# Attention in turns of four steps on 64x64 tiles, with the values' PSUM banks lent to the stages between turns

## The chip, the cores and the metric

One core of one Trainium2 chip. The metric is the device time of one execution in microseconds (us). Engines: PE (TensorE matmul), PEld (its weight loads, which overlap PE), DVE (VectorE), ACT (ScalarE), POOL (GpSimd), SP (DMA queue). PSUM is the memory for matmul results, shared out in banks; the program uses eight.

## The reference, cut to what matters

Layer 0 is a graph convolution with two batch norms over all batches; it is finished 880 us into the kernel and the change does not touch it. Then, for each of 16 batches of `x` (1024 x 256, fp32):

```python
x = layernorm(x + layer0(x))
fea = x.T; c = fea.mean(0)                         # per node
A = abs(abs(sigmoid(c[None] - c[:, None]) - .5) - .5) * 2
g = relu((fea @ (adj * (A + A.T) / 2)) * para)     # -> q, 4 heads of 64
k, v = split(x @ kv_w)
out = softmax(q @ k.T * scale) @ v                 # per head
x = layernorm(x + out)
```

## The kernel before

One instruction stream holds three batches at once: attention of batch b, the graph product, keys and values of b+1, the first layer norm of b+2. Attention of a batch is 16 *steps*. A step takes one pair of heads, one half of the queries (512) and two blocks of 128 keys; four steps make one output tile `o`. The tile names in the profile: `s` scores, `e` their exponentials (ACT), `acc` the sums of e (DVE), `o` the values product, `ot` its copy, `pd`/`dt` the denominators, `pr` their transposes, `pf`/`r` the transposed output and the last layer norm, `yt`/`py`/`px` the first layer norm and its transposes, `wg`/`pg` the graph product, `pk`, `pv` keys and values.

```python
ps_s = pool("ps_s", 2, space=PSUM)      # two tiles of two banks
ps_o = pool("ps_o", 1, space=PSUM)
ps_t = pool("ps_t", 3, space=PSUM)      # everything else
...
def scores(g):                          # contraction over HD = 64 rows
    for a in range(2):
        cb = 2 * cp + a
        t = ps_s.tile([P, 2, FB], F32, tag="s", name=f"s{g}_{a}")
        for h in range(2):              # two 64x128 tiles, one per head
            nc.tensor.matmul(t[:, h, :], kTs[b, pair][h * HD : (h + 1) * HD, ts(cb, P)],
                             qTs[b, pair, hf][h * HD : (h + 1) * HD, :], start=True, stop=True)
...
def attend(g):                          # 64 output columns per head
    for a in range(2):
        for h in range(2):              # two 128x64 tiles
            nc.tensor.matmul(O[b, hf, pair][h * HD : (h + 1) * HD, :],
                             vs[b][:, cb, pair * P + h * HD : pair * P + (h + 1) * HD],
                             E[g, a][:, h, :], start=(cb == 0), stop=(cb == NT - 1))
    if cp == NT // 2 - 1:
        nc.scalar.copy(t, O.pop((b, hf, pair)))
...
for k in range(KB // 2):                # pieces are put into eight slots a batch
    put(b, t + 1 + k, finish_a, b, hf * (KB // 2) + k)   # pf, r, statistics; POOL makes nm
    put(b, t + 2 + k, finish_b, b, hf * (KB // 2) + k)   # ACT: r <- r, nm, rs; store
...
put(b - 2, j + 1, bn2, b, j)            # ACT: yt <- yt
put(b - 2, j + 2, ln1_a, b, j)          # PE: py <- yt, then DVE
...
for t in ...:                           # a slot: s, block of pieces, s, o
    scores(g + 2); exps(g + 2)
    sums(g)
    for f, a in now:
        f(*a)                           # the slot's block of other stages
    sums(g + 1)
    scores(g + 3); exps(g + 3)
    for k in live:
        attend(k)                       # g and g + 1
```

The order of emission is the order on each engine.

Of the kernel before, what the change touches and what calls it, by code (L numbers as in the profile page):

```python
# [9 lines left out]
F32 = mybir.dt.float32  # L10
# [3 lines left out]
PSUM = bass.MemoryType.PSUM  # L14
DRAM = bass.MemoryType.DRAM

P = 128
# [5 lines left out]
def gnn_norm_attention_kernel(  # L23
# [16 lines left out]
    nc = tc.nc  # L40
    B, N, C = x.shape
    H = W1.shape[0]
    NT = N // P
    CT = C // P
    HT = H // P
    FB = 512
    NH = N // FB
    HD = C // HEADS
# [38 lines left out]
    with ExitStack() as l0:  # L87
# [29 lines left out]
        with ExitStack() as ph1:  # L117
# [9 lines left out]
            for i in range(0, NT, 2):  # L127
                t = hp.tile([P, 2, N], F32, tag="h", name=f"A{i}")
# [281 lines left out]
    def fast():  # L410
      with ExitStack() as fx:
        pool = lambda name, bufs, **k: fx.enter_context(tc.tile_pool(name=name, bufs=bufs, **k))
# [10 lines left out]
        sm = pool("sm", 6)  # L423
        rp = pool("rp", 2)
        ps_s = pool("ps_s", 2, space=PSUM)
        ps_o = pool("ps_o", 1, space=PSUM)
        ps_t = pool("ps_t", 3, space=PSUM)

        x1s, x1Ts, css, crows, mvs, wgs = {}, {}, {}, {}, {}, {}
        kTs, qTs, vs, S, E, ACC, O, OT, DT = {}, {}, {}, {}, {}, {}, {}, {}, {}  # L430
# [121 lines left out]
                nc.vector.tensor_scalar(qs, qs, 0.0, scale, op0=OP.max, op1=OP.mult)  # L552


        def step(g):
            b, s = divmod(g, NS)
            hf, pair, cp = s // (NP * NT // 2), s // (NT // 2) % NP, s % (NT // 2)
            return b, hf, pair, cp

        def scores(g):  # L560
            b, hf, pair, cp = step(g)
            for a in range(2):
                cb = 2 * cp + a
                t = ps_s.tile([P, 2, FB], F32, tag="s", name=f"s{g}_{a}")
                for h in range(2):
                    nc.tensor.matmul(  # L566
                        t[:, h, :],
                        kTs[b, pair][h * HD : (h + 1) * HD, ts(cb, P)],
                        qTs[b, pair, hf][h * HD : (h + 1) * HD, :],
                        start=True,  # L570
                        stop=True,
                    )
                S[g, a] = t

        def exps(g):
            for a in range(2):
                E[g, a] = ep.tile([P, 2, FB], F32, tag="e", name=f"e{g}_{a}")
                nc.scalar.activation(E[g, a], S.pop((g, a)), AF.Exp)  # L578

        def sums(g):  # L580
            b, hf, pair, cp = step(g)
            if cp == 0:
                ACC[b, hf, pair] = accp.tile([P, 2, FB], F32, tag="acc", name=f"acc{g}")
                nc.vector.tensor_add(ACC[b, hf, pair], E[g, 0], E[g, 1])  # L584
            else:
                for a in range(2):
                    nc.vector.tensor_add(ACC[b, hf, pair], ACC[b, hf, pair], E[g, a])  # L587

        def attend(g):
            b, hf, pair, cp = step(g)  # L590
            if cp == 0:
                O[b, hf, pair] = ps_o.tile([P, FB], F32, tag="o", name=f"o{g}")
            for a in range(2):
                cb = 2 * cp + a
                for h in range(2):
                    nc.tensor.matmul(  # L596
                        O[b, hf, pair][h * HD : (h + 1) * HD, :],
                        vs[b][:, cb, pair * P + h * HD : pair * P + (h + 1) * HD],
                        E[g, a][:, h, :],
                        start=(cb == 0),  # L600
                        stop=(cb == NT - 1),
                    )
                E.pop((g, a))
            if cp == NT // 2 - 1:
                t = otp.tile([P, FB], F32, tag=f"ot{pair}", bufs=2 - pair, name=f"ot{g}")
                nc.scalar.copy(t, O.pop((b, hf, pair)))
                OT[b, hf, pair] = t

        def dens(b, hf):
# [83 lines left out]
        at = {}  # L693
# [7 lines left out]
        for b in range(B):  # L701

            for hf in range(NH):
                t = (hf + 1) * (NC // NH)
# [25 lines left out]
            for t, n in enumerate(KV):  # L730
                for _ in range(n):
                    f, a = kv.pop(0)
# [9 lines left out]
        nsteps = B * NS  # L742
# [4 lines left out]
        short = (dens, recips, finish_a, x1_t, ln1_a, crow)  # L747
        long = (keys, values, graph)

        def spread(few, many):  # L750

            res, done = [], 0
            for k, fa in enumerate(few):
                upto = len(many) * (k + 1) // (len(few) + 1)
                res += many[done:upto] + [fa]
                done = upto
            return res + many[done:]

        def arrange(pieces):
            first = [fa for fa in pieces if fa[0] is dens]  # L760
            gate = [fa for fa in pieces if fa[0] in (wg_a, wg_b)]
            many = [fa for fa in pieces if fa[0] in long]
            few = [fa for fa in pieces if fa not in first + gate + many]
            few.sort(key=lambda fa: rank.get(fa[0], len(rank)))
            few_pe = [fa for fa in few if fa[0] in short]
            order = spread(many, few_pe) if len(many) < len(few_pe) else spread(few_pe, many)
            if few_pe and many and order[0][0] in long:
                order.remove(few_pe[0])
                order.insert(0, few_pe[0])

            for fa in few:
                if fa[0] not in short:
                    at_ = 0
                    for k, o in enumerate(order):
                        if o[0] in rank and rank[o[0]] <= rank.get(fa[0], len(rank)):
                            at_ = k + 1
                    order.insert(at_, fa)
            pairs = [gate[k : k + 2] for k in range(0, len(gate), 2)]
            res = spread(order, pairs) if order else pairs
            flat = []  # L780
            for o in res:
                flat += o if isinstance(o, list) else [o]
            return first + flat

        for t in range(min(at), max(max(at), nsteps // 2 - 1) + 1):
            g = 2 * t
            now = arrange(at.get(t, []))
            live = [k for k in (g, g + 1) if 0 <= k < nsteps]
            ahead = [k for k in (g + 2, g + 3) if 0 <= k < nsteps]
            if ahead:  # L790
                scores(g + 2)
                exps(g + 2)
            while now and now[0][0] is dens:
                f, a = now.pop(0)
                f(*a)
            if live:
                sums(g)
            if not now and live:
                attend(g)
                live.pop(0)  # L800
                sums(g + 1)
            for f, a in now:
                f(*a)
            if now and live:
                sums(g + 1)
            if ahead:
                scores(g + 3)
                exps(g + 3)
            for k in live:
                attend(k)  # L810

        return nc.values_load(
            badi[0][0:1, 0:1],
# [3 lines left out]
        )  # L817

    flag = fast()


# [149 lines left out]
```

## Time and profile before

| | before |
|---|---|
| median of the first 3 runs | 2670.9 us (2669.99 to 2672.18) |
| PE busy | 2617.7 us, 98% of the span |
| DVE, ACT busy | 1383.0, 1213.4 us |
| one batch with all stages | 110.6 us, 13 of them; the first one took 108.8 |
| shared PSUM banks beside s and o | 3 |

"Busy" of PE is the union of matmul records, which overlap; the prediction therefore reads starts, not busy times. In a timeline row the columns are start, length of the merged group, engine, line, operation, tiles, shapes, count, and in brackets the idle time before it with what ended it. A matmul in fp32 leaves two records.

### The profile page before, as it was taken

Reading aid. Unit: us, or ns where it says so; the run is one execution under the profiler, and the core shown is the slowest. Engines: PE = TensorE matmul, PEld = TensorE weight load, DVE = VectorE, ACT = ScalarE, POOL = GpSimd, SP = SyncE. Lnnn points to the kernel's source line nnn. Section 1 sums busy time; section 2 is a strip of 40 time slices with the busy share of each in tenths; the row PEclk is TensorE's granted clock in tenths of the full one; section 3 lists DMA queues with packets and bytes.
Section 4 is the critical chain, followed back from the end, with each engine's and each line's share of the span. In section 5 each row is a group of like instructions: output and inputs, shape, how many; then the busy total and the mean of one; then the engine's idle time right before and its main releaser. Section 6 shows DMA issues by size and latency. Waiting matters only on the chain.

```text
span 2669.0 us, 24421 instructions
## 1 busy us (share of the span) xinstructions
PE 2617.7 (98%) x9081; PEld 1117.4 (42%) x9081; DVE 1383.0 (52%) x2198; ACT 1213.4 (45%) x1635; POOL 331.5 (12%) x464
## 2 busy tenths in 40 slices
PE   8999999999998899999999999999999999999997
PEld 4444444444444444443444434444344443444432
DVE  5222222223222465765757657576575765757556
ACT  2111111114554464564655646556465564655634
POOL 1110111000000100210102101021011110111102
PEclk9999999999999999999999999999999999999999
DMA  3212222222863111011010100101100011010000
GB/s 126 95 72 84 81 95 79 79 110 71 322 226 113 34 38 32 28 46 39 24 32 28 52 32 24 32 28 52 32 24 32 28 52 32 24 32 28 20 8 25
DMA packets 93789, 161.10 MB, mean 60 GB/s; under 512 B 7656, under 2 KB 73824, under 8 KB 86752
## 3 DMA queue, kind: packets, MB, share of 16 engines
q1 hardware_dynamic: 93664, 159.48, 17.1%
q8 instruction: 73, 1.20, 0.2%
q14 instruction: 52, 0.43, 0.1%
HBM read 97.53 MB, written 61.93 MB: 60 GB/s over the span
## 4 chain that ended last, share of the span: by engine, by line
PE 90%; DVE 5%; ACT 2%; issue 2%; DMA 0%; POOL 0%; SPq 0%; DVEq 0%; ACTq 0%; POOLq 0%
PE s L566 16%; PE pg L546 16%; PE o L596 15%; PE pa L263 14%; PE po L361 8%; PE ph L284 8%; PE pk L520 4%; PE pv L531 2%; PE px L470 1%; PE pd L615 1%; PE pa L247 1%; PE py L447 1%; DVE acc L587 1%; DVE wg L512 1%; DVE r L640 1%
## 5 line engine op out<-in xcount | busy, mean ns | idle before, releaser
L578 ACT ACTIVATE e<-s 128x1024 f32<-128x1024 f32 x512 | 499.0, 1021 | 577.1 <-PE o L596 414.9
L566 PE MATMUL s<-qT,kT 64*128 64x512 f32 x2048 | 508.9, 615 | 0.5 <-ACT e L578 0.5
L587 DVE TENSOR_TENSOR acc<-acc,e 128x1024 f32<-128x1024 f32 x384 | 469.6, 1223 | 19.6 <-DVE acc L587 1.4
L546 PE MATMUL pg<-wg,x 128*128 128x512 f32 x1024 | 467.2, 593 | 1.7 <-DVE wg L512 1.4
L596 PE MATMUL o<-e,v 128*64 128x512 f32 x2048 | 467.7, 598 | 0.0
L566 PEld LDWEIGHTS s<-qT,kT 64*128 64x128 f32 x2048 | 176.0, 186 | 307.4 <-issue 183.0
L303 ACT COPY hT<-ph 128x512 f32<-128x512 f32 x128 | 75.0, 586 | 453.7 <-PE ph L284 453.7
L596 PEld LDWEIGHTS o<-e,v 128*64 128x64 f32 x2048 | 135.5, 136 | 316.5 <-issue 315.4
L546 PEld LDWEIGHTS pg<-wg,x 128*128 128x128 f32 x1024 | 181.3, 190 | 174.6 <-issue 170.3
L512 DVE SCALAR_TENSOR_TENSOR wg<-wg,adj_sb 128x1024 f32<-128x1024 f32 x128 | 156.4, 1222 | 149.5 <-ACT wg L508 145.7
L284 PE MATMUL ph<-agg,W1T 128*128 128x512 f32 x512 | 222.2, 592 | 0.0
L361 PE MATMUL po<-hL,W2T 128*128 128x512 f32 x432 | 185.6, 592 | 0.0
L66 POOL TENSOR_SCALAR rs_z<-mv_z 128x2 f32<-128x2 f32 x64 | 24.0, 375 | 1097.4 <-DVE mv_z L402 1096.4
L304 DVE BATCH_NORM_STATS2 st<-ph 128x6 f32<-128x512 f32 x128 | 89.5, 699 | 136.6 <-ACT hT L303 136.6
L263 PE MATMUL pa<-T,sx 128*128 128x512 f32 x360 | 156.9, 592 | 0.0
L284 PEld LDWEIGHTS ph<-agg,W1T 128*128 128x128 f32 x512 | 97.3, 190 | 122.5 <-issue 122.2
L584 DVE TENSOR_TENSOR acc<-e,e 128x1024 f32<-128x1024 f32 x64 | 78.2, 1222 | 127.5 <-PE pd L615 127.5
L551 DVE TENSOR_TENSOR qT<-pg,para_sb 128x512 f32<-128x512 f32 x64 | 43.8, 684 | 192.7 <-PE pg L546 192.7
L365 DVE BATCH_NORM_STATS2 st<-po 128x6 f32<-128x512 f32 x64 | 44.7, 699 | 169.3 <-PE po L361 169.3
L361 PEld LDWEIGHTS po<-hL,W2T 128*128 128x128 f32 x432 | 82.1, 190 | 103.3 <-issue 103.3
L531 PE MATMUL pv<-kvw,x1T 128*128 128x256 f32 x512 | 121.7, 382 | 3.1 <-DVE r L640 3.1
L520 PE MATMUL pk<-x1T,kvw 128*128 128x512 f32 x256 | 116.9, 600 | 0.0
(133 smaller groups left out, 2475.6 us busy)
## 6 DMA issues: line engine op xcount, KB each, us to landing
h<-hT SPq DMA_DIRECT2D x27, 1024.0 KB, 3.8
hL<-h SPq DMA_DIRECT2D x27, 1024.0 KB, 8.7
x<-in_x_dram SPq DMA_DIRECT2D x16, 1024.0 KB, 5.0
yT<-y SPq DMA_DIRECT2D x32, 512.0 KB, 3.7
yt<-yT SPq DMA_DIRECT2D x64, 256.0 KB, 3.3
xr<-in_x_dram SPq DMA_DIRECT2D x64, 256.0 KB, 4.8
out_dram<-r SPq DMA_DIRECT2D x64, 256.0 KB, 2.1
crow<-crow_d SPq DMA_DIRECT2D x15, 512.0 KB, 4.1
```

Of the source, the lines that this page charges most:

```text
L263: nc.tensor.matmul(p, w[:, k, :], m[:, k, :], start=(k == 0), stop=(k == KN - 1))
L284: nc.tensor.matmul(p, W1T[:, k, ts(f, P)], aggT[b][:, k, ts(h, FB)], start=(k == 0), stop=(k == CT - 1),)
L304: nc.vector.bn_stats(st1[:, f, u, :], p)
L361: nc.tensor.matmul(po[c], W2T[:, k, ts(c, P)], hT[u][:, k, :], start=(k == 0), stop=(k == HT - 1))
L512: nc.vector.scalar_tensor_tensor(t, t, 1.0, adj_sb[:, i, :], op0=OP.add, op1=OP.mult)
L520: nc.tensor.matmul(p, kvw[:, k, ts(c, P)], x1Ts[b][:, k, ts(h, FB)], start=(k == 0), stop=(k == CT - 1))
L531: nc.tensor.matmul(p[:, ts(a, C)], x1Ts[b][:, k, ts(j + a, P)], kvw[:, k, C:], start=(k == 0), stop=(k == CT - 1),)
L546: nc.tensor.matmul(pg[b], x1s[b, k // 2][:, k % 2, ts(c, P)], wgs[b, k][:, ts(h, FB)], start=(k == 0), stop=(k == NT - 1))
L566: nc.tensor.matmul(t[:, h, :], kTs[b, pair][h * HD : (h + 1) * HD, ts(cb, P)], qTs[b, pair, hf][h * HD : (h + 1) * HD, :], start=True, sto ...
L578: nc.scalar.activation(E[g, a], S.pop((g, a)), AF.Exp)
L587: nc.vector.tensor_add(ACC[b, hf, pair], ACC[b, hf, pair], E[g, a])
L596: nc.tensor.matmul(O[b, hf, pair][h * HD : (h + 1) * HD, :], vs[b][:, cb, pair * P + h * HD : pair * P + (h + 1) * HD], E[g, a][:, h, :], ...
```

## The change

Its intent: s and o both use four 64x64 tiles, so that PE need not change its tile shape between them, and four steps stand together (a *turn*) behind one *block* of the other stages, so that shapes change only twice per turn. Each row half of the values product is given a bank of its own, and the halves are added (the prediction says why); the two banks come from the shared pool, which has them for the block.

```diff
-        ps_o = pool("ps_o", 1, space=PSUM)
-        ps_t = pool("ps_t", 3, space=PSUM)
+        ps_t = pool("ps_t", 4, space=PSUM)
 ...  (scores)
-                for h in range(2):
-                    nc.tensor.matmul(
-                        t[:, h, :],
-                        kTs[b, pair][h * HD : (h + 1) * HD, ts(cb, P)],
+                for r in range(2):
+                    for h in range(2):
+                        nc.tensor.matmul(
+                            t[r * HD : (r + 1) * HD, h, :],
+                            kTs[b, pair][h * HD : (h + 1) * HD, ts(2 * cb + r, HD)],
 ...  (attend)
-                O[b, hf, pair] = ps_o.tile([P, FB], F32, tag="o", name=f"o{g}")
+                O[b, hf, pair] = [ps_t.tile([P, FB], F32, tag="t", name=f"o{g}_{r}") for r in range(2)]
+                for r in range(2):
+                    for h in range(2):
+                        nc.tensor.matmul(
+                            O[b, hf, pair][r][h * HD : (h + 1) * HD, :],
+                            vs[b][r * HD : (r + 1) * HD, cb, pair * P + h * HD : pair * P + (h + 1) * HD],
+                            E[g, a][r * HD : (r + 1) * HD, h, :],
 ...
-                nc.scalar.copy(t, O.pop((b, hf, pair)))
+                o = O.pop((b, hf, pair))
+                nc.scalar.copy(t, o[0])
+                nc.vector.tensor_add(t, o[1], t)
 ...  (the loop; the old one goes)
+        NK = NT // 2
+        for t in range(min(at) // 2, max(max(at) // 2, nsteps // NK - 1) + 1):
+            g = NK * t
+            now = arrange(at.get(2 * t, [])) + arrange(at.get(2 * t + 1, []))
 ...         (the block, with sums(g) behind its last short PE piece)
+            for k in range(g, g + NK):
+                if 0 <= k + 1 < nsteps:
+                    scores(k + 1)
+                    exps(k + 1)
+                if 0 <= k < nsteps:
+                    if k > g:
+                        sums(k)
+                    attend(k)
```

More of the change, by code (lines that the diff above doesn't have):

```diff
@@ L564, in scores @@
                 t = ps_s.tile([P, 2, FB], F32, tag="s", name=f"s{g}_{a}")
-                for h in range(2):
-                    nc.tensor.matmul(
-                        t[:, h, :],
-                        kTs[b, pair][h * HD : (h + 1) * HD, ts(cb, P)],
-                        qTs[b, pair, hf][h * HD : (h + 1) * HD, :],
-                        start=True,
-                        stop=True,
-                    )
+                for r in range(2):
[3 more added lines that the diff above has]
+                            kTs[b, pair][h * HD : (h + 1) * HD, ts(2 * cb + r, HD)],
+                            qTs[b, pair, hf][h * HD : (h + 1) * HD, :],
+                            start=True,
+                            stop=True,
+                        )
                 S[g, a] = t
@@ L591, in attend @@
             if cp == 0:
-                O[b, hf, pair] = ps_o.tile([P, FB], F32, tag="o", name=f"o{g}")
+                O[b, hf, pair] = [ps_t.tile([P, FB], F32, tag="t", name=f"o{g}_{r}") for r in range(2)]
             for a in range(2):
                 cb = 2 * cp + a
-                for h in range(2):
-                    nc.tensor.matmul(
-                        O[b, hf, pair][h * HD : (h + 1) * HD, :],
-                        vs[b][:, cb, pair * P + h * HD : pair * P + (h + 1) * HD],
-                        E[g, a][:, h, :],
-                        start=(cb == 0),
-                        stop=(cb == NT - 1),
-                    )
+                for r in range(2):
[4 more added lines that the diff above has]
+                            E[g, a][r * HD : (r + 1) * HD, h, :],
+                            start=(cb == 0),
+                            stop=(cb == NT - 1),
+                        )
                 E.pop((g, a))
@@ L783, in arrange @@
             return first + flat
-        for t in range(min(at), max(max(at), nsteps // 2 - 1) + 1):
-            g = 2 * t
-            now = arrange(at.get(t, []))
-            live = [k for k in (g, g + 1) if 0 <= k < nsteps]
-            ahead = [k for k in (g + 2, g + 3) if 0 <= k < nsteps]
-            if ahead:
-                scores(g + 2)
-                exps(g + 2)
-            while now and now[0][0] is dens:
-                f, a = now.pop(0)
-                f(*a)
-            if live:
-                sums(g)
-            if not now and live:
-                attend(g)
-                live.pop(0)
-                sums(g + 1)
-            for f, a in now:
-                f(*a)
-            if now and live:
-                sums(g + 1)
-            if ahead:
-                scores(g + 3)
-                exps(g + 3)
-            for k in live:
-                attend(k)
+        NK = NT // 2
+        for t in range(min(at) // 2, max(max(at) // 2, nsteps // NK - 1) + 1):
+            g = NK * t
+            now = arrange(at.get(2 * t, [])) + arrange(at.get(2 * t + 1, []))
+            behind = max((k + 1 for k, fa in enumerate(now) if fa[0] in short), default=0)
+            for k in range(len(now) + 1):
+                if k == behind and 0 <= g < nsteps:
+                    sums(g)
+                if k < len(now):
+                    f, a = now[k]
+                    f(*a)
+            for k in range(g, g + NK):
[6 more added lines that the diff above has]
+                    attend(k)
         return nc.values_load(
```

## The prediction

> **What bounds the kernel now.** I read the page first. Its first part and its chain of waits agree on one engine:
>
> ```profile
> PE 2617.7 (98%) x9081; PEld 1117.4 (42%) x9081; DVE 1383.0 (52%) x2198; ACT 1213.4 (45%) x1635; POOL 331.5 (12%) x464
> ...
> PE 90%; DVE 5%; ACT 2%; issue 2%; DMA 0%; POOL 0%; SPq 0%; DVEq 0%; ACTq 0%; POOLq 0%
> PE s L566 16%; PE pg L546 16%; PE o L596 15%; PE pa L263 14%; PE po L361 8%; PE ph L284 8%; PE pk L520 4%; PE pv L531 2%; PE px L470 1%; PE pd L615 1%; PE pa L247 1%; PE py L447 1%; DVE acc L587 1%; DVE wg L512 1%; DVE r L640 1%
> ```
>
> PE bounds; no other engine passes 52%. But 98% busy means only that matmul records touch each other (ends are modelled), so what can be saved inside it must come from start times. The chain of waits in order of time shows pk coming back every 110.6 us from 1046.74 to 2484.51: that is one batch of attention together with the other stages of the next two. Fourteen such batches from 937.91 take 1546.6 us. Before 880 us the change touches nothing.
>
> The windows of one batch (second row) and of the last two, which have less beside attention:
>
> ```profile
> 1267.92:1378.52 110.60, 110.37 (x443) 45.94 (x442) 70.60 (x112) 61.57 (x80) 15.35 (x24) 1.00 0.11 34
> 2484.45:2591.06 106.61, 106.61 (x413) 42.77 (x409) 60.43 (x74) 55.21 (x67) 12.59 (x16) 1.00 0.03 10
> 2591.06:2652.00 60.94, 60.02 (x276) 20.32 (x272) 45.53 (x58) 32.99 (x41) 16.94 (x16) 1.00 0.05 18
> ```
>
> Columns: window, its us, busy PE, PEld, DVE, ACT, POOL, clock, DMA. The clock is full. Now the PE timeline of two of a batch's eight slots:
>
> ```profile
> 1273.20 1.99 PE L566 MATMUL s<-qT,kT 64*128 64x512 f32 x8
> 1275.12 3.65 PE L596 MATMUL o<-e,v 128*64 128x512 f32 x16
> 1278.70 1.99 PE L566 MATMUL s<-qT,kT 64*128 64x512 f32 x8
> 1280.62 0.66 PE L626 MATMUL pr<-ident,dt 128*128 128x128 f32 x4
> 1281.11 1.88 PE L520 MATMUL pk<-x1T,kvw 128*128 128x512 f32 x4
> 1282.83 1.89 PE L531 MATMUL pv<-kvw,x1T 128*128 128x256 f32 x8
> 1284.56 0.60 PE L637 MATMUL pf<-ident,ot 128*128 128x128 f32 x4
> 1285.00 1.89 PE L531 MATMUL pv<-kvw,x1T 128*128 128x256 f32 x8
> 1286.82 1.99 PE L566 MATMUL s<-qT,kT 64*128 64x512 f32 x8
> ```
>
> Read the differences of starts. pk: 1282.83-1281.11 = 1.72 for 4 records, 0.43 each. s: 8 records in 1.92; o: 16 in 3.58. Two records of s (two row halves) and two of o (two column halves) run at once, so s ought to take 4 x 0.43 = 1.71 and o 8 x 0.43 = 3.43. It costs **0.21 us more for each s group, 0.15 to 0.17 for o**, and the block of 128x128 work between them pays about 0.15 (the last pv 1.82 instead of 1.73; pr 0.49 instead of the 0.44 of pf). That is the price of leaving one tile shape and filling the next: about 0.1 out, 0.05 to 0.1 in.
>
> **What the Trainium skill says.** "TensorEngine Tiling (Array Packing)", section Tiling Modes: a change of mode, not of tile, drains the engine; 64x64 gives four tiles that may run together. The trace agrees on the first: every change of form above has its tenth or two, and none stands inside a group. No run yet shows the second for 64x64, but the pd matmuls are four tiles of 128x32:
>
> ```profile
> 1319.80 1.07 PE L615 MATMUL pd<-acc,ones 128*32 128x512 f32 x8
> 1320.80 0.33 PE L470 MATMUL px<-ident,x 128*128 128x128 f32 x1
> ```
>
> Eight records in 1.00 us are two rounds of four and a drain, so four at once works. The same page, section Restrictions and Gotchas: different row tiles must not use one PSUM bank at the same time. That is why the changed values product needs two banks and an addition. "Perfetto Trace Analysis", section Per-engine timelines: ScalarE and VectorE are strict FIFO. The timeline of ACT agrees (an e is done only after the wg and yt work issued before it), and my main worry rests on it.
>
> **The change part by part.** *Removed:* mode changes. A batch now has eight slots of s, block, s, o (twice as many steps as slots): s in and out twice, o once, block once, 0.21+0.21+0.16+0.15 = 0.73, times 8 = 5.8 us. Afterwards s and o are both 64x64 and four steps stand together; a batch has four turns, each with one change in and one out, about 0.29, so 1.2 us. **Saved 4.6 us a batch.** Check: the pure work of a batch is 64 rounds for s, 64 for o, 64 records for pg, 16 for pk (each 0.429: 89.2), 32 for pv (0.216: 6.9), 57 transposes (0.109: 6.2), pd 4 rounds (1.7), 104.0 in all; 110.6 - 104.0 = 6.6, of which the 5.8 is most.
>
> *Added on PE:* 2048 s and 2048 o records more, each a quarter of the array: 16 records of 0.43 us, four at once, take the 1.71 of 8 records two at once. Zero if four do run together, issue included: a round asks for four weight loads and four matmuls in 0.43 us, and the early transposes (30 in 3.56 us at 12.58, less as the clock rises) keep about 0.11 us per pair.
>
> *Added on DVE:* 64 additions from PSUM, 128x512. Row L449, the same kind of addition from PSUM, has 0.68 us, so 44 us of DVE, 1383 to 1427, beside PE. *ACT:* unchanged in work. *PSUM:* eight banks as before, but four for s and four shared in place of four, three shared and one for o; between turns the two of o serve the block. At a block's start one or two of them are free, and o's pair comes free after the ACT copy (0.59) and the DVE addition (0.69), some 1.6 us in, when the order of instructions first asks for them about 1 to 2.8 us in. Hidden, or nearly.
>
> *Moved, and this is where gain is given back:* two slots' pieces are now one block, with no attention between a piece that ACT prepares and the piece that PE does with it. I walked the orders of PE, ACT and DVE through the four blocks with the traced durations (ACT: copy 0.5, 256-wide 0.5, wg even 2.15, wg odd 1.05, e 1.0 when back to back).
> - Block B (second of a batch). PE: pf 0.5, pv 1.73, py 0.44, pv 1.73, done at 4.5, and then py of the next half slot, whose yt comes from ACT. ACT before that: ot to 0.7, two r to 1.7, v not before pv is done at 2.5, to 3.05, wg to 5.2, two yt to 6.3. With its four transposes PE is done at 6.7 instead of 4.9: **1.8 us of stall**. Before, a whole s-o-s stretch lay between.
> - Block A (first). PE 12.4 us (pd, 4 pk, pr, pf, 2 pv). ACT idles while it waits for pk and pv copies, then after the first v (10.85) has wg 2.15, yt 1.0, v 0.5, wg 1.05, so the first e of the turn is done at 16.55, where the second s of the turn wants its bank at 15.9: **0.8 us**.
> - Blocks C and D: ACT has only copies; the DVE chains (L640, L645, statistics, L456) end before PE asks. About 0.
> - Inside a turn: s for step k+1 is 1.71, o for step k 1.71, and e has over 1.2 us of slack. DVE sums 2.5 us a step against 3.42. About 0.
>
> So 2.6 given back, against some 0.4 of small stalls in a batch now: net 110.6 to about 108.1, -2.5. Times 14 = 35 us. Batch 15 (no py, no yt) keeps all 4.6, the last about 3 to 4 of it. The tail has one addition more, +0.7. Sum: 35 + 4.6 + 3.5 - 0.7 = 42, thus **2670.9 - 42 = 2629 us, -1.6%**.
>
> **The rivals.** (1) *The moved waits are hidden after all*: the gain is 4.6 to 5 in all 16 batches, 75 us, 2596. For it: the waits of the kernel before are tiny on PE, so the author's order is good. Against: block B's sum above is plain arithmetic on a FIFO. (2) *Four 64x64 tiles do not keep four at once*, because 2 x 18.7 instructions per us are not issued or fetched, or weight loads of one row half wait for each other. For: no run shows a long stretch of it; only the short pd and early transposes come near. Each 10% on the 55 us of s and o in a batch would be 5.5 us x 16 = 88 us, so 2715. Against: pd shows rounds of four at full pace, o and s each show the two halves free. (3) *PSUM becomes the wait*: o's two banks are held until DVE has added, and DVE is behind by its block work. A microsecond at each of 64 turns would be 64 us and cancel everything: 2690. Against: DVE in the walk is free within 1.5 us of each turn's end. (4) *ACT becomes the bound of whole turns*, if block A leaves it 3 us or more late: some 20 to 40 us more.
>
> **Range and chances.** The mode saving is firm (70 us if undisturbed); the give-back is 28 us by the walk, perhaps 0 to 60. That makes 2600 to 2668. Faster by over 2% needs under 2617.5, i.e. a give-back below about 18 us: 0.30. Slower by 2% needs rival 2: 0.07.
>
> **What would show it.** In the PE timeline of a batch, s and o should be one unbroken stretch of 13.7 us per turn, 128 records, with starts of a round 0.43 apart: the mode step and the four-at-once step. If it is longer with idle marked "issue", rival 2; if ended by ACT e inside the turn's first step, block A's estimate (or rival 4). A gap of about 1.8 us before py in the second block, ended by ACT yt, is the block B step; its absence makes me wrong towards 2600. Waits of PE for the DVE addition or the ACT copy of ot would be rival 3. The batch period should be near 108.1 us; 106 says rival 1, 110 or more says 2 or 3. DVE busy should rise by 44 us, ACT not at all, and nothing before 880 us should move.

## The result, and the profile after

| | before | after |
|---|---|---|
| median | 2671.54 us (4 runs) | 2641.41 us (4 runs; 2638.72 to 2642.31) |
| ratio | | 0.9886, 95% interval 0.9869 to 0.9903 |
| one batch | 110.60 us | 108.20 us |
| PE / DVE / ACT busy | 2617.7 / 1383.0 / 1213.4 | 2560.5 / 1426.4 / 1218.5 |

A ratio is the mean time of one kernel's fast runs over that of the other's of the same rounds, so not quite the ratio of the medians. The change gains 1.1%, clear of noise. All outputs are right.

From the page of the changed kernel (busy time by engine, and the chain that ended last by engine):

```profile
PE 2560.5 (97%) x13177; PEld 1114.8 (42%) x13177; DVE 1426.4 (54%) x2262; ACT 1218.5 (46%) x1635; POOL 346.4 (13%) x464
...
PE 90%; ACT 4%; DVE 3%; issue 1%; POOL 1%; DMA 0%; SPq 0%; ACTq 0%; DVEq 0%; POOLq 0%
```

PE has 4096 records more and still bounds; DVE is up by 43 us, as 64 additions should make it. ACT's share of the chain rises from 2% to 4%. Where it stands there, the PE timeline of the second block of a batch and of the ends of the turns around it tells:

```profile
1269.73 1.90 PE L599 MATMUL o<-e,v 64*64 64x512 f32 x16
1272.10 2.00 PE L568 MATMUL s<-qT,kT 64*64 64x512 f32 x16 [0.47 <-ACT e L580]
1273.91 1.90 PE L599 MATMUL o<-e,v 64*64 64x512 f32 x16
1275.63 1.90 PE L568 MATMUL s<-qT,kT 64*64 64x512 f32 x16
...
1282.61 0.66 PE L642 MATMUL pf<-ident,ot 128*128 128x128 f32 x4
1283.10 1.89 PE L530 MATMUL pv<-kvw,x1T 128*128 128x256 f32 x8
1284.83 0.60 PE L446 MATMUL py<-ident,yt 128*128 128x128 f32 x4
1285.27 1.89 PE L530 MATMUL pv<-kvw,x1T 128*128 128x256 f32 x8
1288.30 0.33 PE L446 MATMUL py<-ident,yt 128*128 128x128 f32 x1 [1.14 <-ACT yt L436]
1288.79 0.55 PE L446 MATMUL py<-ident,yt 128*128 128x128 f32 x3 [0.16 <-ACT yt L436]
```

Starts again: o 1273.91 to s 1275.63 is 1.72 us for 16 records, four rounds of 0.43 with nothing between o and s. Four tiles do run at once, and the change of shape inside the turn is gone. But s at 1272.10 came 0.65 us late by the starts (1269.73 + 1.72 is 1271.45; 0.47 of it shows as idle, for e) and py at 1288.30 came 1.3 us late: pv starts at 1285.27 and takes 1.73, so py could start at 1287.00. ACT's timeline of the same stretch:

```profile
1283.19 1.09 ACT L662 ACTIVATE r<-r,nm,rs_z 128x256 f32<-128x256 f32 x2
1285.03 0.59 ACT L537 COPY v<-pv 128x512 f32<-128x512 f32 x1 [0.75 <-PE pv L530]
1285.51 1.15 ACT L506 ACTIVATE wg<-crow,cs 128x1024 f32<-128x1024 f32 x1
1286.70 1.06 ACT L507 ACTIVATE wg<-wg 128x1024 f32<-128x1024 f32 x1
1287.66 1.08 ACT L436 ACTIVATE yt<-yt,t,s 128x256 f32<-128x256 f32 x2
```

ACT idles 0.75 us for pv, does 2.1 us of wg, and only then the yt that PE waits for. It is not short of time; it is a queue in an unlucky order.

To see where a batch's time goes I took, from the starts of its matmul records, the distance from each group of one tile to the next, less the pure work (0.429 us per record of 512 columns on the whole array, half or a quarter of that on two or four tiles, 0.216 for pv, 0.109 for a transpose). The pure work is 104.1 us in both kernels:

| extra in one batch, us | before | after |
|---|---|---|
| between s and o | 2.79 | 0.92 (about 0.7 of it goes with the late e) |
| from s or o to the block | 1.60 | 0.44 |
| from the block to s | 0.97 | 0.39 |
| waits for yt (before: of pv for a bank) | 0.40 | 1.68 |
| the rest (pd, fills inside the block) | 0.71 | 0.64 |
| sum | 6.47 | 4.07 |

That explains the full batches. It does not explain the end. In the span of the trace, the kernel is ahead by 2.1 us when the first of these batches starts, gains 4.4 in that one and 31.1 in the next 13 - 37.6 in all - and gives back 7.8 after 2446.85. The PE timeline of the last batch, where only short pieces are left between the turns:

```profile
2566.06 1.95 PE L568 MATMUL s<-qT,kT 64*64 64x512 f32 x16
2567.83 1.90 PE L599 MATMUL o<-e,v 64*64 64x512 f32 x16
2573.85 3.69 PE L568 MATMUL s<-qT,kT 64*64 64x512 f32 x16 [4.12 <-ACT e L580]
2577.31 2.84 PE L599 MATMUL o<-e,v 64*64 64x512 f32 x16
2579.98 1.89 PE L568 MATMUL s<-qT,kT 64*64 64x512 f32 x16
```

What ACT did meanwhile (timeline):

```profile
2571.80 1.09 ACT L662 ACTIVATE r<-r,nm,rs_z 128x256 f32<-128x256 f32 x2 [4.64 <-POOL nm L654]
2572.80 1.91 ACT L580 ACTIVATE e<-s 128x1024 f32<-128x1024 f32 x2
```

The clock of the two stretches from the window view; behind the window, its length and the busy times of PE, PEld, DVE, ACT and POOL stand granted clock, DMA share and GB/s:

```profile
2573.80:2580.00 6.20, 6.15 (x36) 1.94 (x40) 4.90 (x4) 2.96 (x3) 0.00 (x0) 0.56 0.12 42
2580.00:2587.00 7.00, 7.00 (x72) 2.18 (x68) 2.45 (x2) 3.88 (x4) 0.00 (x0) 1.00 0.00 0
```

ACT stood 4.64 us in front of an r whose nm POOL had not finished, with e behind it in the queue. PE idled 4.1 us, and then ran at half its clock (the 0.56 is a mean over a window that reaches past the slow stretch; the window 2572.40:2579.23 alone shows 0.50): s took 3.46 us from start to start in place of 1.72, the o after it 2.67. The same happens at 2607. Against whole turns at full clock the two places cost 7.0 and 6.7 us (idle 4.3 and 4.4, the rest the slow clock).

### The profile page after: what moved, and what is told of

The parts are those of the page before. It is cut to its first block, busy times and chain, and to the rows that moved or that the text cites. A ratio compares the mean times of both kernels' runs of the same rounds, so it can differ in the third digit from the quotient of the medians.

```text
span 2639.1 us, 32959 instructions
## 1 busy us (share of the span) xinstructions
PE 2560.5 (97%) x13177; PEld 1114.8 (42%) x13177; DVE 1426.4 (54%) x2262; ACT 1218.5 (46%) x1635; POOL 346.4 (13%) x464
## 3 DMA queue, kind: packets, MB, share of 16 engines
q8 instruction: 105, 1.72, 0.3%
## 4 chain that ended last, share of the span: by engine, by line
PE 90%; ACT 4%; DVE 3%; issue 1%; POOL 1%; DMA 0%; SPq 0%; ACTq 0%; DVEq 0%; POOLq 0%
PE pg L545 16%; PE s L568 16%; PE o L599 16%; PE pa L263 14%; PE po L361 8%; PE ph L284 8%; PE pk L519 4%; PE pv L530 1%; PE pd L620 1%; PE px L469 1%; PE pa L247 1%; PE py L446 1%; ACT yt L436 1%; ACT wg L506 1%; ACT wg L502 1%
## 5 line engine op out<-in xcount | busy, mean ns | idle before, releaser
L568 PE MATMUL s<-qT,kT 64*64 64x512 f32 x4096 | 493.8, 597 | 14.9 <-ACT e L580 14.9
L599 PE MATMUL o<-e,v 64*64 64x512 f32 x4096 | 486.8, 591 | 0.0
L568 PEld LDWEIGHTS s<-qT,kT 64*64 64x64 f32 x4096 | 147.7, 133 | 311.2 <-issue 266.3
L599 PEld LDWEIGHTS o<-e,v 64*64 64x64 f32 x4096 | 157.1, 134 | 285.4 <-issue 276.9
L66 POOL TENSOR_SCALAR rs_z<-mv_z 128x2 f32<-128x2 f32 x64 | 41.0, 641 | 1047.8 <-DVE mv_z L402 1025.9
L470 ACT COPY x1T<-px 128x512 f32<-128x512 f32 x64 | 37.5, 586 | 194.6 <-PE px L469 194.6
L611 DVE TENSOR_TENSOR ot<-o,ot 128x512 f32<-128x512 f32 x64 | 44.3, 691 | 136.5 <-ACT ot L610 135.1
```

Source lines behind the costliest of these rows:

```text
L568: nc.tensor.matmul(t[r * HD : (r + 1) * HD, h, :], kTs[b, pair][h * HD : (h + 1) * HD, ts(2 * cb + r, HD)], qTs[b, pair, hf][h * HD : (h + ...
L599: nc.tensor.matmul(O[b, hf, pair][r][h * HD : (h + 1) * HD, :], vs[b][r * HD : (r + 1) * HD, cb, pair * P + h * HD : pair * P + (h + 1) * HD],
```

## The experiments

The theory after the result: (1) one shape for s and o saves about 4.3 us a batch; (2) merging two slots into one block puts three ACT pieces into a bad place in its queue: yt before py, a late wg and yt before e, and r before its nm; (3) each is an order of issue, not a lack of ACT time, and can be moved. The rivals: the turns save and not the shapes; PSUM is what PE waits for; PE is throttled at the end for a reason of its own. The kernels of a set ran on one chip beside the kernel before, with three timed rounds each: first the four moves below, then three more. The changed kernel was not timed again in these sets; the kernel before was, and its median stayed at 2671.5 us, so times are compared across the sets.

### r one block later

```diff
-                    put(b, t + 2 + k, finish_b, b, hf * (KB // 2) + k)
+                    put(b, t + 2 + 2 * k, finish_b, b, hf * (KB // 2) + k)
```

> Change: the ACT pieces that normalise r of the second half of each pair (finish_b, k=1) are issued one block later than in the changed kernel, nothing else. Theory: in the last batch, blocks are so short that ACT sits 4.6 us in its FIFO waiting for POOL's nm, with the e of the turn behind it; PE idles 4.2 us twice, and then runs at about half clock for another 2.4 and 2.7 us. So 14 us go, all of it after 2540 us: 2641 -> about 2627; the batch period stays 108.2; the two waits of s for e over 4 us and the granted clock of 0.56 to 0.60 behind them are gone. Rival: PE is throttled there for a reason of its own (long dense 64x64 turns), or the wait only moves to another piece: time stays within 4 us of 2641.

Measured: 2626.76 us (ratio 0.9835, interval 0.9818 to 0.9851), 14.6 us under the changed kernel. The batch period stays 108.20. From the start of the last pk (the keys of the sixteenth batch) to the end of the span it took 177.7 us in place of 192.3. The same place of the last batch, PE timeline:

```profile
2566.29 1.90 PE L599 MATMUL o<-e,v 64*64 64x512 f32 x16
2568.01 1.90 PE L568 MATMUL s<-qT,kT 64*64 64x512 f32 x16
```

The window around it, in the columns as above:

```profile
2565.00:2575.00 10.00, 10.00 (x100) 3.64 (x96) 9.34 (x13) 6.43 (x8) 4.83 (x4) 1.00 0.08 28
```

No wait, and full clock: this slow clock was a consequence of the idle time, not a property of long 64x64 stretches. The rival falls.

### yt first in its block, quarters 1 and 3

```diff
             now = arrange(at.get(2 * t, [])) + arrange(at.get(2 * t + 1, []))
+            early = [fa for fa in now if (fa[0] is bn2 and fa[1][1] in (1, 3)) or (fa[0] is load and fa[1][1] == 0)]
+            now = early + [fa for fa in now if fa not in early]
```

> Change: the ACT pieces that scale yt of the quarters 1 and 3 are issued first in their block instead of behind the wg pieces. Theory: py in the second block of a batch waits for yt in the ACT FIFO (1.3 + 0.16 us a batch). The gap before py goes: period 108.2 -> about 106.7, 14 batches, -20 us: about 2621. Rival: py would wait as long for its PSUM bank (an eviction by DVE) or the stall moves to the next piece (v copies issued later): gain under 5 us.

(The edit also issues one load early, that of quarter 0.)

Measured: 2616.53 us (0.9795, 0.9779 to 0.9812), 24.9 under the changed kernel; period 106.46, so 1.74 us a batch. That is more than expected: the expectation counted the idle time of 1.46 us, and by the starts the delay was 1.68. The PE timeline at the same place:

```profile
1281.91 1.89 PE L530 MATMUL pv<-kvw,x1T 128*128 128x256 f32 x8
1283.64 0.60 PE L446 MATMUL py<-ident,yt 128*128 128x128 f32 x4
```

py follows pv after 1.73 us, so py's PSUM bank was free by then.

### yt first, quarter 0

The same edit with `fa[1][1] in (0,)`.

> Change: load and scaling of yt quarter 0 are issued first in the first block of a batch (where ACT idles while it waits for pk), not between its wg pieces. Theory: the second s of the first turn waits 0.5 to 0.65 us because e is behind 5 us of ACT work, 1.0 us of it this yt. That wait goes: period 108.2 -> about 107.6, -7 to -9 us: about 2633. Rival: the wait is set by the last wg, which cannot start before v, and only shifts: under 2 us.

Measured: 2629.04 us (0.9843, 0.9826 to 0.9859), 12.4 under the changed kernel. The period is 107.45, 0.75 us a batch or 9.8 us over 13 batches, a little more than expected. Another 2.4 us came before the first of those batches (it starts at 933.39 in place of 935.77), which nobody had expected. The window view of the same stretch, the changed kernel first and this run below it, shows that the clock is behind it:

```profile
903.28:910.12 6.84, 6.33 (x10) 2.52 (x10) 2.16 (x3) 0.15 (x1) 0.00 (x0) 0.50 0.00 0
903.28:910.12 6.84, 5.79 (x16) 2.21 (x14) 4.45 (x10) 0.58 (x2) 0.00 (x1) 1.00 0.00 0
```

At half clock six pg records of the changed kernel took 5.28 us; here they took 2.68. The move is not needed for that: the run with r one block later moves no yt and has full clock there too. PE had just waited 1.15 and 0.69 us in the changed kernel, and 1.16 and 0.70 here, so what made the clock fall only there is not shown. Thirteen of the fourteen short waits of s for e are gone; the two long ones at the end remain, as they should, but cost 6.1 and 6.2 us in place of 7.0 and 6.7, because half clock lasted 3.4 us behind each and not 6.8. Each of these traces is of one execution.

### All three moves

> All three moves together. If the three causes are separate, the gains add: -14 -20 -8 = -42, about 2599 us, period about 106.1, which would be 2.7% below the kernel before. If they share one cause (ACT is simply short of time after a block), the sum falls clearly short, above 2610.

Measured: 2597.31 us (0.9724, 0.9708 to 0.974), 2.8% faster than the kernel before and 44.1 us under the changed one. The three single gains add up to 51.9. The period is 106.00 in most batches, where the sum of the two single gains would give 105.7. The missing 0.3 is visible in the second block: its six pg products take 5.53 us to the next s and not the 5.15 of pure work plus 0.1; the last one now comes before its wg is ready (ACT, then DVE). So a part of the waits was hidden behind one another, but most of it was separate. This 0.3 x 13 is 4 us of the 8 that the sum misses. Part of the rest is the clock: the stretch of half clock at 903 us in the changed kernel's trace is missing in two of the single runs and half as long in the third, so the sum can count it more than once. How much that is in the timed runs stays open.

### The old shapes in the new order

The loop and the PSUM pool of the changed kernel, with `scores` and `attend` of the kernel before (one shared bank for o, no addition).

> Change: the changed kernel's order (turns of four steps behind one block), but s on 64x128 and o on 128x64 as before, one bank for o and no DVE addition. Theory: the gain comes from s and o having one tile shape, so every s-to-o and o-to-s step inside a turn costs its 0.15 to 0.2 us again: 8 groups of s and o a turn cost 4 x 0.21 + 4 x 0.16 against 0.15 now, +5.2 us a batch less what hides in the waits for ACT (0.65). Period 108.2 -> 112.8 to 113.4, time about 2710 to 2725, slower than the kernel before too. Rival: it is the grouping into turns that saves (fewer passes between attention and the other stages), the shape adds nothing: within 10 us of 2641.

Measured: 2712.67 us (1.0156 of the kernel before, 1.0139 to 1.0173); period 112.83. PE timeline of a turn:

```profile
1287.13 1.94 PE L597 MATMUL o<-e,v 128*64 128x512 f32 x8
1288.99 1.99 PE L567 MATMUL s<-qT,kT 64*128 64x512 f32 x8
1290.91 1.94 PE L597 MATMUL o<-e,v 128*64 128x512 f32 x8
```

o takes 1.86 and s 1.92 us from start to start where four rounds are 1.72. By the same accounting the extra between s and o is 5.4 us a batch, against 0.9 with 64x64. The rival "turns alone" is dead: turns in the old shapes cost more than the old order, because each step then changes the shape twice. The same waits for yt (1.7 us a batch) appear here too, so they belong to the order, not to the tiles.

### The new shapes in the old order

The kernel before with the changed `scores` and `attend`, `ps_o` of two banks and `ps_t` of two.

> Change: the order of the kernel before (two steps a slot around a block), but s and o on 64x64, with two banks of their own for o and only two shared ones. Theory of shapes: o to s needs no change of mode, so a slot has two changes (0.29) in place of four (0.73): 3.5 us a batch saved if two shared banks suffice, period 110.6 -> 107.1, about 2615; and no ACT waits in the last batch. Rival: with pg open only one shared bank is left, and PE waits for each eviction; then the period is 110 or more (2660 and up), and this is why the change brings the turns: they let o's banks serve the block.

Measured: 2668.65 us (0.999, 0.9973 to 1.0007): no gain; period 110.60, to the hundredth that of the kernel before. The accounting says why. The changes of shape fell as the theory of shapes has it: between s and o from 2.8 to 0.4 us a batch, from s to the block from 1.6 to 0.9. The waits in the block rose. The waits of PE: who waited for whom (total us, times, longest):

```profile
PE py L447 <- DVE r L644: 15.1, 13, 1.2
PE px L470 <- ACT dt L621: 10.2, 14, 0.7
PE pg L546 <- DVE qT L551: 8.0, 16, 0.5
...
PE pv L531 <- ACT v L538: 4.5, 15, 1.1
```

Each of these is released by an eviction, and most come once a batch. The four shown sum to 37.8 us in 58 waits. In the kernel before, the only one of this kind that comes every batch is pv behind r, 3.1 us in 13 waits. So some 34.7 us in 14 batches, 2.5 us a batch, took the place of the 3.1 us that the shapes had saved; the other half microsecond I have not traced. In the last two batches, which have less beside attention, this run is faster than the kernel before: from the last pk to the end 179.2 us against 184.5, though it starts them 3.5 us later. The rival of the expectation held. The 64x64 form as written takes one bank more for o, and here takes it from the block; the turns give it back. No run tests the old order with more shared banks: all eight are in use.

### r last in its block, with all three moves

```diff
+            end = [fa for fa in now if fa[0] is finish_b]
+            now = early + [fa for fa in now if fa not in early + end] + end
```

> All three moves as in all3, and the ACT pieces that normalise r stand last in their block. In all3 the last piece of pg in the second block still waits 0.29 us a batch for wg 5 (ACT then DVE), which is why its gains did not quite add. With r behind the wg pieces, wg comes 1 us earlier: that wait goes, period 106.0 -> 105.7, 2597 -> about 2593. Rival: e of the next turn is then delayed by r and the gain is lost: 2597 or more.

Measured: 2602.68 us (0.9744, 0.9728 to 0.976), 5.4 us more than without this step: a miss for the theory, and the rival of the expectation. The pg products run to the next s without a wait again, but in the first block r now stands directly before e, and s waits 0.46 us for e there as in the changed kernel. The period is 106.46. The best version measured is the one with the three moves, 2597.31 us.

## Why the prediction was right, and where a term was off

- **The saving of shape changes** (4.6 us a batch): right, and slightly too high. The table has 5.36 us of shape-change extra before (2.79 + 1.60 + 0.97) where the prediction counted 5.8, and after the change 1.75, of which about 0.7 goes with the late e: 1.05 where it counted 1.2. Saved: 4.3.
- **Four tiles at once**: right, 0.43 us a round through whole turns; rival 2 did not happen.
- **Block B**, 1.8 us of stall before py: the table has 1.7. **Block A**, 0.8 us: 0.65 by the starts, and 0.75 a batch when the cause is removed. (The walk's own times, 16.55 and 15.9, differ by 0.65; the 0.8 is a slip.) **Blocks C, D and the inside of a turn**, 0: right. The batch period came out at 108.20 against about 108.1.
- **PSUM** (rival 3): no wait of PE for the copy or the addition of o shows in this order. In the old order, with two shared banks, waits for evictions took back what the shapes had saved; that run supports the credit that the prediction gave to the lent banks. Rival 4 did not happen either: the late e costs one step of the first turn, and the rest of the turn has no wait.
- **The end was mis-sized, and with its sign.** The prediction's term was "Batch 15 (no py, no yt) keeps all 4.6, the last about 3 to 4 of it. The tail has one addition more, +0.7", a gain of 7.4 us. Measured is a loss of 7.8. The walk through ACT's queue was done for a full batch, where r's nm comes while PE has 10 us of other work, and was not repeated for the last batch, where PE has half a microsecond of block work (pf) before the next s. There ACT waited for POOL 4.6 us, twice; PE idled over 4 us, and the slow clock behind it cost another two to three: 13.7 us in all. Three waits of pr for dt, 0.7 us each, where the kernel before has one, are another 1.4, and so nearly all of the 15.2 that lie between the two signs is found. Moving these pieces of r gave 14.6 us. Part of the miss was met from the other side, by luck, for the sum had no term for it: the ramp gained 2.1 us and the first batch 4.4 where the sum had 2.5. So 2641 in place of 2629, inside the range.
- **Slips that decided nothing**: "2 x 18.7 instructions per us" counts twice; 16 records and 16 weight loads in 1.72 us are 18.7 together. A give-back of 0 to 60 us from a saving of 70 ends at 2661, not 2668.

On the skill: the drain on a change of mode that "TensorEngine Tiling (Array Packing)", section Tiling Modes, states is seen both ways here, 0.15 to 0.2 us with it and under 0.02 us from s to o without it. "TensorE: Matmul & The Clock Gate", section Part 1: The HAM clock gate, says that PE's clock is halved after an idle window of about 3.4 us. The trace agrees for the long waits: after 4.1 us of idle it was granted 0.56 over the next 6.2 us, and a round took 0.85 us in place of 0.43; the waits of 0.5 and 1.3 us in a batch left it at 1.00. But one long wait is not needed: at 903 us it was halved in the changed kernel after waits of 1.15 and 0.69 us, and in another run after the same two waits it was not.

## What to carry to other kernels

Count the changes of tile shape on PE before counting matmuls: two forms that fill the array equally well still cost 0.15 to 0.2 us here at every change between them, and making their shapes equal paid although it took an extra bank and an addition, once the bank could be borrowed. When pieces are merged into longer blocks, walk each in-order queue anew, and not only in the steady state: a piece that was far enough from its producer may now stand in front of what the bounding engine needs, and the shortest block (here the last batch) is the one to check. The stalls of 4.3 us cost 6.1 to 7.0 here, with the slow clock behind them, so look at the clock wherever PE stood still. Look at it also where a run gains or loses a few microseconds that nobody expected.

## What the Trainium skill lacked or had wrong

- "TensorEngine Tiling (Array Packing)" says that a change of mode drains, but gives no cost. Measured: 0.20 us from 64x128 to 128x64, 0.15 back, 0.20 from 64x128 to 128x128, 0.11 from 64x64 to 128x128, about 0.1 from 128x128 to a tiled form (0.15 to 64x64, with the first step from s to o).
- The same page says that row tiling increases PSUM pressure; what that is worth is not there. Measured: with two shared banks in place of three, nothing was left of some 3.1 us a batch that the shapes had saved (period 110.60 in both), and 2.5 us of it are found in waits for evictions.
- "TensorE: Matmul & The Clock Gate", Part 3, has no 64x64 row among its measured speedups. Measured: 16 records on four 64x64 tiles take 1.72 us, a quarter of 16 times the 0.43 us of one record on the whole array, over turns of 128 records, with a weight load before each. No run has 64x64 records one at a time.
- The same part lists that weight loads overlap running matmuls only when the row group differs, although its own paragraph on the mechanism allows a background weight buffer too. The "only" does not fit the traces: in the kernel before, o's tiles of 128 rows share all rows, and rounds of 0.43 us follow each other though each has weight loads of 0.14 us; so do the 64x64 rounds.
- "Perfetto Trace Analysis" says that PE's end times are a model, but not how far off they can be. Measured: groups listed with 1.90 us follow each other at 1.72 us; only starts can be used for costs of this size.
